# Layer 1's norms and features follow the gathering of expert results, its weights are prepared before the experts, and one edge input is read from PSUM

## The chip, the core and the metric

The kernel runs on one core of a Trainium2 chip. The core has five engines that each take their own instructions in order: TensorE (PE in the profile, with PEld for its weight loads), VectorE (DVE), ScalarE (ACT), GpSimd (POOL) and SyncE (SP), and 16 DMA engines that move data between the chip's memory and the core's two on-chip memories, SBUF and PSUM. The metric is the device time of one execution in microseconds (us), lower is better. The time before the change is 2966.57 us, the median of 3 runs (2961.47 to 2970.36).

## What is computed

A graph network of two layers over 3125 nodes with 256 features and 53125 edges. Each layer is a graph step and a feed-forward step, and each step adds to x what it makes of the normalised x:

```python
x = x + _L0_gnn_ref(_layernorm(x, axis=-1), edge_index, edge_weight, ...)   # 4 attention heads
x = x + _L0_ffn_ref(_layernorm(x, axis=-1)[None], ...)[0]                   # 16 experts, best 2 per node
x = x + _L1_gnn_ref(_layernorm(x, axis=-1), ..., src, dst, edge_type_200)   # 200 relations
x = x + _L1_ffn_ref(_layernorm(x, axis=-1)[None], ...)[0]                   # half of the nodes
```

Layer 0's graph step weighs each edge, per head, and takes a weighted mean over the edges of a node:

```python
score = a_s[:, src] + a_d[:, dst] + aw_e[:, None] * elem[None, :] + ab[:, None]
w = jnp.exp(-jax.nn.relu(score / 20.0))
pooled = jax.vmap(lambda wi, fi: seg(wi[:, None] * fi))(w, dst_f)
row_sum = jax.vmap(lambda wi: seg(wi))(w)
out = pooled / row_sum[:, :, None]
```

Layer 1's graph step has one weight per edge, made from both nodes and the edge's relation. The score's vector is the product of a 768 x 768 matrix W3 and a vector a. Since each alpha is divided by a sum over its own single entry, an edge's message is its source's features plus its relation's, times alpha / alpha:

```python
W = (W3 @ a)[:, 0]
score = h[src] @ w_src + h[dst] @ w_dst + rel_e @ w_rel
alpha = jnp.exp(jax.nn.leaky_relu(score))[:, None]
alpha = alpha / jnp.sum(alpha, axis=1, keepdims=True)
msg = (h[src] + rel_e) @ weight_neighbor * alpha
agg = jax.ops.segment_sum(msg, dst, num_segments=n)
node_repr = jax.nn.relu(agg) + loop_message
```

## The kernel before

Nodes lie in 25 tiles of 128 partitions; x (25 x 256 f32 per partition) stays in SBUF. Edges are sorted on the chip by target node, so that tile b of nodes owns 18 tiles of 128 edges (the last owns 8): 440 edge tiles, taken in 74 groups of six (GRP, the last of two). The program goes through these stages in order of time: sorting for layer 0; node features and edges of layer 0; sorting for layer 1, prepared; the experts, into which the moves of layer 1's sorting are woven; features of layer 1; edges of layer 1; the last feed-forward step.

A scheduler in the compiler orders the instructions of each engine from the program's order and a model of their times, and adds the waits. On the chip each engine then keeps its order: an instruction that waits holds all behind it on its engine. Buffers of a pool come free when their last user is done. Pools that are opened after others were closed lie in the memory that these left.

**Edges of a layer** (`edge_stages`, run by `pipelined` as a three-step pipeline over the groups):

- `gather`: GpSimd issues six indirect DMAs, one per edge tile, that fetch the rows of 128 edges from a table in DRAM into `rows`, which has three buffers (L733). VectorE makes the one-hot of the target node, `oh`, by comparing `iota` with the edges' target in its tile (L741), both read from SBUF. It also makes `hot` in bf16 by comparing `wide`, the same targets laid along the free axis and broadcast to all partitions, with the partition's number (L750). Layer 0 has one `hot` per group, layer 1 three (one for the target, two for the relation). `wide` is loaded once per node tile by SyncE, as one run of 18 x 128 values per partition (L722 to L725); layer 1 loads two.
- `message`: TensorE picks each edge's target score with `hot` (L759), VectorE sums the parts (L765), and then `messages` of the layer follows. Layer 0 (`heads_edges`): the score (L891 to L893), Exp on ScalarE into `msg` (L895), and the product of the row's 4 x 64 values with the four weights (L896), both inputs in SBUF. Layer 1 (`relations_edges`): the score (L1242), the weight, ScalarE's scaling of `oh` by it into `ohw` (L1251), and the one-hot of the relation, from `iota` and the edge's relation, both in SBUF, written beside the row (L1245).
- `add`: TensorE sums the group's messages into the tile's accumulator in PSUM, `ps_sum`, one of two buffers (L776). After a tile's last group VectorE takes it out (L784) and `finish` adds to x: L907 to L910 in layer 0; in layer 1 a chain over TensorE, ScalarE and VectorE (L1262 to L1287).

**Experts** (`experts`): norms of x, gate logits (L945), gating, 50 scatters of the nodes' places (L1014), then 65 tiles of work, each with its expert's weights loaded by SyncE. At the end GpSimd gathers for each node tile its two expert results, `yg` (L1102, six buffers), and VectorE adds them to x (L1106).

**Features of layer 1** (`relations_features`, called after the experts): W3 and a are loaded (L1130) and multiplied by rows, which gives W3 a (L1135); then the relation weights through TensorE (L1154 to L1185); then `layer_norm` of all 25 tiles (L149 to L156), whose Sqrt and reciprocal are one instruction each for all tiles and so need the last tile; then per tile two transposes, a copy, four matmuls and a copy into `f` (L167, L169, L1196, L1200), and one write to the table per five tiles (L1202).

## Time and profile before

| what | value |
|---|---|
| median of 3 runs | 2966.57 us |
| the profiled execution's own time | 2936.63 us |
| its span in the trace | 2934.5 us |
| TensorE, VectorE, GpSimd busy | 1868.3 us (64%), 1397.0 us (48%), 1416.7 us (48%) |
| gathers of rows (L733) | 880, mean 1118 ns |
| edges of layer 0, first to last gather's end | 397.1 to 1040.7 us |
| first expert's tokens gathered, last expert's result | 1335.8 to 1841.7 us |
| gathering of expert results | 1844.6 to 1906.9 us |
| edges of layer 1, first gather's start to last one's start | 1991.2 to 2636.9 us |

A line of the timeline gives the start in us from the span's start, the duration, the engine, the line of the program, the operation, its output and inputs, their shapes, how many were merged, and in brackets how long the engine sat idle before it and what ended that. A line of the chain of waits gives start, duration and what the program's end was waiting for then. In the table of stretches each engine has its busy time with the number of instructions in brackets, then the granted TensorE clock (1 is full), the share of the DMA engines that is busy, and GB/s. "issue" as the reason for a gap means that the engine waited for nothing that the profile shows.

### The profile page before, as it was taken

What the parts mean: (1) busy time and instruction counts of PE and PEld (TensorE: products, weight loads), DVE (VectorE), ACT (ScalarE), POOL (GpSimd) and SP (SyncE); (2) the same over time, 40 slices, a digit from 0 to 9 for tenths busy, and PEclk for the clock granted to TensorE, in tenths of its full rate; (3) what the DMA queues carried; (4) which work ended last, traced back from release to release, by engine and by line L of the source; (5) the groups of instructions that cost most, each with busy time, mean ns of one, the idle gap of its engine ahead of it and who ended that gap; (6) DMA issues with size and microseconds to landing.
All of it is one profiled execution on the core that took longest, in us unless ns stands there. A gap on an engine that the chain in (4) does not pass through costs nothing.

```text
span 2934.5 us, 24129 instructions
## 1 busy us (share of the span) xinstructions
PE 1868.3 (64%) x7420; PEld 1114.8 (38%) x7420; DVE 1397.0 (48%) x3320; ACT 368.6 (13%) x1008; POOL 1416.7 (48%) x1291
## 2 busy tenths in 40 slices
PE   3079644545455442406999999055877887786298
PEld 0024333333343310304666666042444444343166
DVE  4976344444444448423442222444555555548811
ACT  0000100000000000100002222011222222222012
POOL 4435247877777743154441111606777777760000
PEclk9999967766777755556779999587889888998599
DMA  2040144443444320004449998325555545530000
GB/s 80 0 128 5 35 130 119 117 120 111 122 117 117 100 74 0 1 0 152 127 128 314 314 317 280 93 88 165 147 148 146 149 137 148 148 101 33 7 20 17
DMA packets 185930, 334.13 MB, mean 114 GB/s; under 512 B 32733, under 2 KB 109799, under 8 KB 185799
## 3 DMA queue, kind: packets, MB, share of 16 engines
q1 hardware_dynamic: 122919, 191.33, 19.9%
q0 software_dynamic: 53520, 132.71, 17.0%
q10 hardware_dynamic: 9360, 8.52, 0.8%
q8 instruction: 60, 0.98, 0.1%
q14 instruction: 71, 0.58, 0.1%
HBM read 298.41 MB, written 34.04 MB: 113 GB/s over the span
## 4 chain that ended last, share of the span: by engine, by line
PE 29%; DVE 8%; POOL 7%; DMA 5%; issue 4%; ACT 1%; SPq 0%; DVEq 0%; ACTq 0%; POOLq 0%
PE ps_h L1062 8%; POOL rows L733 7%; PE ps_y L1079 4%; PE ps_sum L776 3%; DMA rows<-table,s_idx 3%; PE s_mv L550 3%; DVE cmp L1358 3%; PE ps_hid L1385 3%; PE ps_out L1396 2%; DMA yg<-ytab,moe_pi 1%; PE ps_h_t L167 1%; PE ps_loop L1275 1%; PE ps_f L1196 1%; DVE hot L750 1%; PE ps_x_t L167 1%
## 5 line engine op out<-in xcount | busy, mean ns | idle before, releaser
L733 POOL DMA_INDIRECT rows<-table,s_idx x880 | 983.5, 1118 | 462.5 <-issue 246.5
L776 PE MATMUL ps_sum<-rows,ohw 128*128 128x457 f32 x880 | 416.8, 618 | 117.1 <-ACT ohw L1251 116.8
L776 PE MATMUL ps_sum<-msg,oh 128*128 128x260 f32 x880 | 303.0, 519 | 135.0 <-DVE msg L896 135.0
L550 PE MATMUL s_mv<-s_hv,s_hp 128*128 128x200 f16 (+1 forms) x832 | 246.6, 471 | 88.5 <-DVE s_hv L545 88.5
L776 PEld LDWEIGHTS ps_sum<-msg,oh 128*128 128x128 f32 x880 | 229.1, 267 | 192.1 <-DVE msg L896 141.4
L776 PEld LDWEIGHTS ps_sum<-rows,ohw 128*128 128x128 f32 x880 | 173.7, 210 | 275.6 <-ACT ohw L1251 169.8
L1062 PE MATMUL ps_h<-w,x_t 128*128 128x512 f32 x520 | 255.4, 637 | 0.0
L1051 POOL DMA_INDIRECT xg<-xtab,who x65 | 62.0, 954 | 310.7 <-PE ps_x_t L167 295.0
L550 PEld LDWEIGHTS <-s_hp 128*128 128x128 f16 x832 | 121.9, 147 | 207.5 <-issue 91.8
L559 POOL DMA_INDIRECT s_tab<-s_rec,s_to x130 | 147.2, 1132 | 102.3 <-ACT s_rec L556 67.0
L891 DVE TENSOR_TENSOR s<-near,rows 128x24 f32<-128x24 f32 x74 | 13.5, 183 | 362.5 <-DMA rows<-table,s_idx 344.9
L741 DVE TENSOR_TENSOR oh<-iota,s_row 128x768 f32<-128x768 f32 (+1 forms) x148 | 138.6, 937 | 45.4 <-ACT ohw L1251 45.4
L759 PEld LDWEIGHTS <-hot 128*128 128x128 bf16 x1760 | 57.9, 98 | 269.3 <-DVE near L765 179.7
L1251 ACT ACTIVATE ohw<-oh,s 128x128 f32<-128x128 f32 x440 | 136.5, 389 | 105.3 <-DVE ln_mv L150 53.8
L759 PE MATMUL ps_near<-near0p,hot 128*128 128x12 bf16 x440 | 22.8, 174 | 198.7 <-DVE near L765 162.9
L1068 DVE TENSOR_TENSOR hid<-hid,ps_h 128x512 f32<-128x512 f32 x65 | 44.7, 687 | 210.6 <-ACT hid L1067 210.6
L1062 PEld LDWEIGHTS ps_h<-w,x_t 128*128 128x128 f32 x520 | 102.7, 209 | 104.7 <-issue 104.5
L437 POOL TENSOR_TENSOR s_pos<-s_pos,s_own 128x416 f32<-128x416 f32 x50 | 72.0, 1439 | 143.9 <-DVE s_own L434 124.5
L896 DVE TENSOR_TENSOR msg<-rows,msg 128x1536 f32<-128x1536 f32 x74 | 128.2, 1734 | 1.3 <-ACT msg L895 0.4
L1079 PE MATMUL ps_y<-w,h_t 128*128 128x256 f32 x520 | 122.9, 379 | 0.7 <-ACT h_t L169 0.7
L750 DVE TENSOR_SCALAR hot<-wide,pcols 128x768 bf16<-128x768 bf16 (+1 forms) x296 | 120.4, 423 | 3.3 <-DMA wide<-s_w 3.3
L1079 PEld LDWEIGHTS ps_y<-w,h_t 128*128 128x128 f32 x520 | 98.7, 190 | 41.7 <-issue 30.6
(293 smaller groups left out, 2495.7 us busy)
## 6 DMA issues: line engine op xcount, KB each, us to landing
w<-in_L_ffn_w_dram SPq DMA_DIRECT2D x195, 512.0 KB
wide<-s_w SPq DMA_DIRECT2D x72, 576.0 KB
rows<-table,s_idx POOLq DMA_INDIRECT x880
ytab<-y ACTq DMA_DIRECT2D x65, 128.0 KB
sums<-sums_z SPq DMA_DIRECT2D x5, 1142.5 KB
more<-sums SPq DMA_DIRECT2D x25, 228.5 KB
sums<-sums_z SPq DMA_DIRECT2D x5, 650.0 KB
table<-f SPq DMA_DIRECT2D x5, 650.0 KB
```

What stands on the lines that cost most here:

```text
L550: nc.tensor.matmul(ps[:, : NK * V], hp[:, :, j], rec[:, :, :, j].rearrange("p k v -> p (k v)"), start=(j0 + j == 0), stop=(j0 + j == C - 1),)
L559: d = nc.gpsimd.indirect_dma_start(out=tab, out_offset=bass.IndirectOffsetOnAxis(ap=to[:, i : i + 1], axis=0), in_=out[:, k * CH * V : (k ...
L733: nc.gpsimd.indirect_dma_start(out=rows[:, j, :width], out_offset=None, in_=table, in_offset=bass.IndirectOffsetOnAxis(ap=st["idx"][:, k + ...
L741: nc.vector.tensor_tensor(oh[:, :n, :], self.iota[:, None, :P].to_broadcast(sh), st["row"][:, k : k + n, None].to_broadcast(sh), op=OP.is_ ...
L750: nc.vector.tensor_scalar(t[:, : n * P], w, at, None, op0=OP.is_equal)
L776: nc.tensor.matmul(ps[:, :W], oh[:, j, :], msg[:, j, :], start=(head and j == 0), stop=(last and j == n - 1),)
L896: nc.vector.tensor_tensor(msg[:, :n, :HO].rearrange("p j (h o) -> p j h o", o=O), rows[:, :n, :HO].rearrange("p j (h o) -> p j h o", o=O), ...
L1062: nc.tensor.matmul(ph[:, i * HID : (i + 1) * HID], xt[:, c, :], w12[:, i, c, :], start=(c == 0), stop=(c == C - 1),)
L1079: nc.tensor.matmul(py[:, :D], ht[:, c, :], w3[:, c, :], start=(c == 0), stop=(c == HC - 1))
L1251: nc.scalar.activation(ow[:, j, :], oh[:, j, :], AF.Copy, scale=s[:, 1, j : j + 1])
L1358: nc.vector.tensor_scalar(cmp[:, s:e], wrow[:, s:e], w, None, op0=op, op1=OP.add, accum_out=rank[:, t, i : i + 1],)
L1385: nc.tensor.matmul(ph[:, : nt * P], w1[:, c, f * P : (f + 1) * P], zt[:, c, : nt * P], start=(c == 0), stop=(c == C - 1),)
```

## The change

Three edits go together.

**One edge input from PSUM.** `edge_stages` takes the two big PSUM buffers for the whole stage. `hold` gets a copy of the first 256 values of `iota` in its first bank (`numbers`) and in its second the edge weights of layer 0 (`weights_ps`); `sums2` holds the two accumulators, one bank each, by the tile's parity. `oh` and the one-hot of the relation compare `numbers`. In layer 0 ScalarE makes Exp twice, once into PSUM for the product and once into `msg`.

```diff
+        hold, sums2 = self.ps_a("ps_hold"), self.ps_a("ps_sums")
+        numbers = hold[:, :256]
+        nc.vector.tensor_copy(numbers, self.iota[:, :256])
+        self.numbers, self.weights_ps = numbers, hold[:, 512:]
...
-                oh[:, :n, :], self.iota[:, None, :P].to_broadcast(sh),
+                oh[:, :n, :], numbers[:, None, :P].to_broadcast(sh),
...
-                now["sum"] = self.ps_a("ps_sum")
+                now["sum"] = sums2[:, b % 2 * 512 : (b % 2 + 1) * 512]
...
+                w = self.weights_ps[:, : n * H].rearrange("p (j h) -> p j h", h=H)
+                nc.scalar.activation(w, s, AF.Exp)
                 nc.scalar.activation(msg[:, :n, HO:], s, AF.Exp)
...
-                    msg[:, :n, HO:, None].to_broadcast([P, n, H, O]), op=OP.mult,
+                    w[:, :, :, None].to_broadcast([P, n, H, O]), op=OP.mult,
...
-                    rows[:, :n, R0:], self.iota[:, None, :R].to_broadcast(sh),
+                    rows[:, :n, R0:], self.numbers[:, None, :R].to_broadcast(sh),
```

With it `wide` is laid in pieces of two edge tiles (256 values) with 8 values of room behind each, and `hot` is made from it in that form:

```diff
-            t = pool.tile([P, self.tiles[0] * P], BF16, name=f"wide{i}")
+            t = pool.tile([P, self.tiles[0] // 2, 2 * P + 8], BF16, name=f"wide{i}")
...
-                w = now[b][min(i, 1)][:, lo : lo + n * P]
-                t = pool.tile([P, G * P], BF16, name=f"hot{i}", bufs=3)
-                nc.vector.tensor_scalar(t[:, : n * P], w, at, None, op0=OP.is_equal)
+                w = now[b][min(i, 1)][:, lo : lo + n // 2, : 2 * P]
+                t = pool.tile([P, G // 2, 2 * P], BF16, name=f"hot{i}", bufs=3)
+                nc.vector.tensor_scalar(t[:, : n // 2, :], w, at, None, op0=OP.is_equal)
```

**Weights ahead of the experts.** `relations_features` becomes a generator. Its first part, up to the relation weights, is called after layer 1's sorting is prepared and before `experts`. W3 and a lie in a pool of their own that is closed at once; the pool of the features stays open through the experts.

```diff
-                self.experts(steps)
-        self.relations_features()
+                features = self.relations_features()
+                self.experts(steps, next(features))
+                next(features, None)
```

**Norms and features tile by tile.** `layer_norm` is split, so that `norm_tiles` makes the statistics, Sqrt, reciprocal and the normalised values of some tiles. `experts` calls `done(t)` after a tile's two additions, and at the ends of groups (4, 4, 4, 4, 4, 2 and 3 tiles) `done` makes norms, features and the table's write for the group.

```diff
+                done(t)
...
+            ends = list(range(4, NT - 4, 4)) + [NT - 3, NT]
+
+            def done(b):
+                if b + 1 not in ends:
+                    return
+                i = ends.index(b + 1)
+                t0, t1 = ends[i - 1] if i else 0, b + 1
+                self.norm_tiles(self.h1, t0, t1)
                 f = pool.tile([P, 5, D + 2], F32, name="f1")
-                n = min(5, NT - t0)
-                for t in range(t0, t0 + n):
+                for t in range(t0, t1):
...
+            yield done
```

## The prediction

> **What bounds the kernel now.** I read the table of stretches (busy time by engine) first: the two edge stages, 397 to 1041 us and 1991 to 2637 us, hold 44% of the span. Then GpSimd's own records there, one `rows` gather per 128 edges:
>
> ```profile
> core 0: us, POOL busy (x), PEclk, DMA share, GB/s
> 330.00:1050.00 720.00, 509.80 (x440) 0.71 0.39 112
> 1985.00:2640.00 655.00, 473.75 (x440) 0.87 0.51 144
> ```
>
> Both stages issue 440 gathers. The median gather takes 0.949 us, so 440 need 417.6 us. Layer 0 spends 92.2 us above that, layer 1 56.2 us. The timeline shows from whom:
>
> ```profile
> 2223.34 0.96 DVE L741 TENSOR_TENSOR oh<-iota,s_row 128x768 f32<-128x768 f32 x1 [1.90 <-ACT ohw L1251]
> 2224.22 0.63 DVE L784 TENSOR_TENSOR acc<-ps_sum,more 128x457 f32<-128x457 f32 x1
> 2224.76 1.40 DVE L1245 TENSOR_TENSOR rows<-iota,s_val 128x1200 f32<-128x1200 f32 x1
> ...
> 2223.98 1.14 POOL L733 DMA_INDIRECT rows<-table,s_idx  x1 [0.30 <-issue]
> 2225.42 1.56 POOL L733 DMA_INDIRECT rows<-table,s_idx  x1 [0.30 <-issue]
> ```
>
> See the ends. The gather begun at 2223.98 ends at 2225.12, 0.82 us after `oh` ended (2224.30). The next ends at 2226.98, 0.82 us after the compare of L1245 (2226.16). A gather that begins inside a VectorE operation with two SBUF inputs starts its work when that ends. L784 has one PSUM and one SBUF input. It ran 2224.22 to 2224.85, across the first gather's start of work, and did not hold it: held, the gather would have ended at 2225.67. That is the row for this change.
>
> In layer 0 GpSimd alone sets the pace: from 400 to 1000 us, 124.3 of the 124.6 us of gaps before gathers are "issue", 0.30 us each. In layer 1 it is not alone: about 55 us of gaps wait for VectorE or TensorE.
>
> Between the stages the chain of waits gives a serial stretch:
>
> ```profile
> 1898.39 2.79 DMA yg<-ytab,moe_pi
> 1902.14 2.79 DMA yg<-ytab,moe_pi
> 1905.90 2.67 DMA yg<-ytab,moe_pi
> 1911.04 7.78 DVE xn L156 x24
> 1918.87 5.37 DVE w3a L1135 x12
> 1925.22 1.80 PE ps_rw L1162 x4
> 1927.67 1.82 PE ps_rw L1162 x4
> 1978.76 3.93 DMA table<-f
> ```
>
> Gathering of expert results, all norms, W3 times a, relation weights, then 25 feature tiles: the last addition to x ends at 1909.15, the last table write issues at 1978.76. That is 69.6 us with GpSimd idle.
>
> **1. One input from PSUM, layer 0.** `oh` (74 times, 0.94 us) and `msg` (74, 1.73 us) get one PSUM input, so by L784 they hold no gather. Still with two SBUF inputs: L909 and L910 (0.41 us per tile each), L891 and L892 (0.18 and 0.16 per group). A gather starting at random inside one of length d waits d/2, with chance d/1.25: 0.067 us per 0.41 us operation, 3.3 us for 49 of them, and 1.7 us for the small ones. Saved: 92.2 - 5 = **87 us** (74 if I am wrong about a fifth, 92 at most). What is late next: a group's gathers then take 7.5 us, VectorE's work 4.0 us (44% of 8.95), TensorE's 4.6; rows has three buffers, so neither is near.
>
> [...] L784 at 260 wide takes 413 ns, L910 at 256 wide, all SBUF, 412. I take 0[...]. ScalarE's second Exp (74 at 0.22 us) finds an engine 2% busy; VectorE waits for the first of the pair, as now.
>
> **2. The same in layer 1.** Here a latency loop decides. A tile's first group takes TensorE from 2195.25 to 2206.65, 11.4 us without a gap, because the finish of the tile before is interleaved. Its rows buffer goes to the next tile's first group: gathers 2206.93 to 2214.7 (7.8 us), landed 2217.99, weights to 2221.35 and TensorE at 2221.90, 26.6 us on. GpSimd waits 1.6 to 2.6 us per tile for that buffer. Freed gathers shorten the loop only by this group's contention, 7.9 to 7.5 us in the tiles I read; the rest becomes a longer wait for the buffer. Against it stands one slower `hot` in the loop (part 3), 0.2 us. Net -0.3 us for 24 tiles: **-7 us**. If the loop did not bind, all 56 us would go; I take the loop.
>
> **3. `hot` and its padded input.** No row shows the new pattern. [...] The source is now 3 x 256 with gaps. [...] Kept: 409 ns as now. Refused: the rows 128x768 (409) and 128x256 (278) give 0.256 ns per element, and half the rate adds 197 ns. On 222 operations in layer 1 that is 44 us of VectorE, in layer 0 (74) 15 us, beside gathers except the one in the loop. I take refused. [...]
>
> Each `wide` copy now lands in 512 B runs. Queue rows: q10 moves 910 B packets in 0.8% of 16 engines (40 ns each), q1 1557 B packets in 76 ns. Two copies per tile are 2304 runs, 144 per engine: 3.2 us at q10's time per byte, 5.8 us at 40 ns per run, against 3.5 now. Per layer-1 tile that is -0.3 to +2.3 us, in a burst (2211 to 2217) under the loop's last gather. q10 is no dearer per byte, so 0; end +55 us.
>
> **4. Weights ahead of the experts.** W3 now loads into the buffers of the finished sorting, and the experts' own tiles lie where W3 was. Before:
>
> ```profile
> 1199.96 0.38 SPq L508 DMA_DIRECT2D s_buckets<-s_bki  x1
> 1208.97 0.37 SPq L928 DMA_DIRECT2D gw<-in_L_ffn_gate_w_dram  x1
> ```
>
> SyncE's gate-weight load waits 9 us for that memory; TensorE, idle 94 us behind it, starts the logits at 1213.07. Logits (27 us), gating, and 50 scatters of 1.26 us follow in series to the first expert, with nothing to hide a shift. In the new order: W3's load (1909.35 to at most 1918.87, 9.5 us), six multiplies to 1924.2, then gw: +14.8 us. SyncE's queue holds W3, a, wx and two `re` loads ahead of gw. The relation matmuls ended 22.0 us after W3's issue; if TensorE keeps them in front, the logits start 17.9 us later. I take **+16 us** (0 if the experts' tiles lie clear of W3, 18).
>
> **5. Norms and features follow the gathering.** GpSimd's 50 gathers (947 ns + 0.30) are 62.6 us, 2.50 us per tile. VectorE per tile by start-to-start times: two additions 0.82, stats 0.49, normalise 0.33, feature copy 0.43, shares of reciprocal and near 0.12, together 2.19 us. It fits, with 0.3 us to spare. Contention: 0.38 x 0.24 us per gather, 4.6 us, and normalising 1; I take 6 us. TensorE: 1.87 us per tile at granted clock 0.99, but the clock in this stretch was 0.51, where transposes took 0.60 instead of 0.38 us and the 256-wide relation matmuls 2.0; so up to 3 us for each of the last three tiles. After the last addition: stats 0.6, Sqrt and reciprocal 1.0, first normalise 0.4, three tiles 9, copies and issue 0.7, together 12 us. 69.6 - 12 - 6 = **-52 us** (-36 to -60). The table's own landing and the record load behind it stay.
>
> **Sum.** -87 - 7 + 16 - 52 = -130 us. The profiled execution took 2936.63 us (span 2934.5 and 2 around it): 2807. The median shown is 2966.57, 1.0% above it, so -131 there: **2835 us**.
>
> **Rivals.**
> A. VectorE becomes the bound while gathering: its queue is in order, and each feature copy waits out a 1.87 us tile. For: 0.3 us slack, six yg buffers. Against: in the trace stats are already woven between additions. 25 x 3.6 = 90 us + 12 saves 30 instead of 52: **2857**.
> B. Layer 1 lengthens: 512 B runs at the dear end plus `hot` in the loop, +62 us instead of the -7. For: the loop. Against: q10. **2900**.
> C. Layer 1's loop does not bind, its 56 us go: **2785**.
> D. Slower. [...] all nine per tile sit on layer 1's loop, 5.3 us, with 2.3 us for the runs: 7.6 x 24.4 = 185 us. It decides from 5.6 us per tile; **about 3026**. Against: runs of 256 adjacent elements, and only one `hot` seen in the loop.
> That the change doesn't do what it says: PSUM next to a broadcast SBUF input might hold gathers still. L784 and L1281 argue against; it falls within D's share.
>
> **Chances.** Forecast 0.50, A 0.17, B 0.15, C 0.06, D 0.12 (a quarter of it within 0.3%, what a measurement here can tell from no change). Faster 0.88, same 0.03, slower 0.09. Range: C and the cheap ends below (2790), B above: 2910. D is left out.
>
> **What would show it.** Right: layer 0's gathers nearly all 0.95 us, its stage near 555 us long; `hot` near 606 ns; GpSimd waiting longer for `rows` in layer 1; gate weights loaded 15 us after the memory is free; the last table write 12 to 20 us after the last addition. Wrong: gathers still ending 0.82 us after `msg`, layer-1 tiles leaving 26 us either way, or additions waiting for feature copies.

## The result and the profile after

The changed kernel takes 2983.76 us (median of 6 runs, 2976.39 to 2995.04). The kernel before, run beside it, takes 2967.39 us (6 runs). The ratio is 1.0062 with a 95% interval of 1.0038 to 1.0087: **slower by 0.6%**. The profiled execution took 2982.18 us, its span 2978.5. The forecast was 2835.

Here are the stages of the two profiled executions, in us. A stage of edges runs from its first `rows` gather to the end of its last. `xg` is the first tile that the experts load, `yg` the first gathering of expert results. The 397 us ahead of layer 0's edges are the same in both.

| stage | before | after | difference |
|---|---|---|---|
| edges, layer 0 | 643.6 | 683.2 | +39.6 |
| to the first `xg` (weights moved here) | 295.1 | 305.3 | +10.2 |
| experts, to the first `yg` | 508.8 | 506.6 | -2.2 |
| `yg` to layer 1's first `rows` gather | 146.6 | 111.3 | -35.3 |
| edges, layer 1 | 647.0 | 678.2 | +31.2 |
| after layer 1's last gather | 296.4 | 296.9 | +0.5 |

The stage that should have lost most of the time gained some. Yet GpSimd's own records in it are as forecast. This is the view of stretches for GpSimd in the changed kernel, over the two edge stages; the columns are the stretch, its length, GpSimd's busy time with the number of instructions, the granted clock, the share of the DMA engines and the rate.

```profile
core 0: us, POOL busy (x), PEclk, DMA share, GB/s
330.00:1090.00 760.00, 419.92 (x440) 0.70 0.38 106
1995.00:2690.00 695.00, 416.05 (x440) 0.86 0.52 135
```

Against 509.80 and 473.75 before, the contention is gone: 440 gathers take 420 and 416 us, 0.95 us each. But the stages contain 263 and 262 us in which GpSimd does nothing. In layer 0 the view of waits says for whom (columns: the waiting instruction, its releaser; total us, number, longest):

```profile
POOL rows L747 <- DVE msg L913: 132.7, 16, 8.6
POOL rows L747 <- issue: 127.9, 417, 1.1
```

"issue" is the 0.30 us per gather that was there before. New are 16 waits of about 8.3 us for `msg`, the last reader of a `rows` buffer. So VectorE was late with `msg`. What VectorE waits for is the next view:

```profile
DVE oh L755 <- remote: 244.7, 22, 17.4
DVE s L906 <- DMA rows<-table,s_idx: 80.4, 23, 5.4
DVE acc L799 <- remote: 24.8, 4, 7.5
DVE oh L755 <- PE ps_sums L791: 18.1, 8, 6.3
```

`oh` of a group has three buffers. It can start when TensorE's sums (L791) three groups earlier have read that buffer. "remote" means that the trace has a semaphore event for the release but no engine's work that ended close to it. The timeline shows what that is (columns: start, duration, engine, line, operation; in brackets the idle time before it and the releaser):

```profile
675.39 1.75 DVE L913 TENSOR_TENSOR msg<-rows,ps_hold 128x1536 f32<-128x1536 f32 x1
677.29 4.39 PE L791 MATMUL ps_sums<-msg,oh 128*128 128x260 f32 x12 [2.47 <-DVE msg L913]
...
686.10 0.95 POOL L747 DMA_INDIRECT rows<-table,s_idx  x1 [0.30 <-issue]
691.66 0.96 DVE L755 TENSOR_TENSOR oh<-ps_hold,s_row 128x768 f32<-128x768 f32 x1 [14.52 <-remote]
```

VectorE ended `msg` at 677.14. TensorE heard of it at once: it started the sums at 677.29, 0.15 us later. The sums that this `oh` waits for are those of an earlier group and had ended at 674.82, before `msg` even began. **VectorE went on at 691.66, 16.84 us after that end**, and 4.6 us after GpSimd had run out of buffers and stopped (its last gather ended at 687.05). Behind `oh` in VectorE's order stood the work that would have given GpSimd its buffer.

By this view it is no wait for an engine's work: TensorE's message that it is done arrives late. (Starts of matmuls are recorded, their ends are modelled, so the trace can't tell a late message from a last matmul that finished late.) In layer 0 of this execution `oh` and `near` wait 32 times for TensorE. Counted from the moment when both the matmul and VectorE's own previous work had ended, these waits make 246 us, 24 of them over 1 us and up to 15.0. The 23 of `oh` among these start 6.6 to 22.0 us after the sums' end. In layer 1 it is `near`:

```profile
DVE near L780 <- remote: 107.4, 24, 9.9
```

In the profile that the prediction was read from there is none of this: in its layer 1 the 22 waits of `near` start at most 0.08 us after the matmul's end, and in its layer 0 neither `oh` nor `near` waits for TensorE.

A second thing is new, and nothing in the forecast allowed for it. The two accumulators in PSUM were two buffers and are now two halves of one, `sums2`. Before, TensorE ran from one tile's sums into the next tile's while VectorE had yet to take out the finished one (`acc`; its buffer is then free). Here are such a change of tile before (24 matmuls are two groups, of two tiles, without a break) and one in the changed kernel (run e12, below):

```profile
594.61 8.39 PE L776 MATMUL ps_sum<-msg,oh 128*128 128x260 f32 x24 [1.66 <-DVE msg L896]
603.02 0.41 DVE L784 TENSOR_TENSOR acc<-ps_sum,more 128x260 f32<-128x260 f32 x1
```

```profile
596.45 0.42 DVE L799 TENSOR_TENSOR acc<-ps_sums,more 128x260 f32<-128x260 f32 x1
597.02 4.75 PE L791 MATMUL ps_sums<-msg,oh 128*128 128x260 f32 x12 [1.76 <-DVE acc L799]
```

In all 24 changes of tile of layer 0 the changed kernel's next sums start 0.14 to 0.15 us after `acc` ends, in the recorded run as in e12. Before, they started 0.3 to 5.8 us ahead of that end, all 24 times. So a TensorE that waits for VectorE's `acc` now stands in a ring with a VectorE that waits for TensorE's sums, once per tile. Every kernel below with the PSUM inputs has this ring.

### The profile page after: what moved, and what is told of

Its sections match the earlier page's. It is cut to its first block, busy times and chain, and to the rows that moved or that the text cites. A ratio compares the mean times of both kernels' runs of the same rounds, so it can differ in the third digit from the quotient of the medians.

```text
span 2978.5 us, 24253 instructions
## 1 busy us (share of the span) xinstructions
PE 1884.8 (63%) x7420; PEld 1116.8 (37%) x7420; DVE 1438.6 (48%) x3330; ACT 377.1 (13%) x1088; POOL 1268.6 (43%) x1291
## 5 line engine op out<-in xcount | busy, mean ns | idle before, releaser
L747 POOL DMA_INDIRECT rows<-table,s_idx x880 | 836.0, 950 | 626.6 <-issue 234.6
L791 PE MATMUL ps_sums<-rows,ohw 128*128 128x457 f32 x880 | 417.9, 622 | 61.9 <-ACT ohw L1280 51.1
L791 PE MATMUL ps_sums<-msg,oh 128*128 128x260 f32 x880 | 299.2, 509 | 166.8 <-issue 87.2
L791 PEld LDWEIGHTS ps_sums<-msg,oh 128*128 128x128 f32 x880 | 222.7, 260 | 219.1 <-issue 154.2
L755 DVE TENSOR_TENSOR oh<-ps_hold,s_row 128x768 f32<-128x768 f32 (+1 forms) x148 | 140.0, 946 | 291.4 <-remote 244.7
L791 PEld LDWEIGHTS ps_sums<-rows,ohw 128*128 128x128 f32 x880 | 180.5, 217 | 219.2 <-issue 158.0
L764 DVE TENSOR_SCALAR hot<-wide,pcols 128x768 bf16<-128x768 bf16 (+1 forms) x296 | 173.7, 592 | 69.6 <-PE ps_near L773 51.4
L773 PEld LDWEIGHTS <-hot 128*128 128x128 bf16 x1760 | 67.5, 98 | 359.8 <-DVE hot L764 214.5
L913 DVE TENSOR_TENSOR msg<-rows,ps_hold 128x1536 f32<-128x1536 f32 x74 | 128.3, 1733 | 0.4
L541 DVE TENSOR_TENSOR s_hp<-num_p,s_pp 128x1024 f16<-128x1024 f16 x104 | 71.8, 690 | 82.7 <-PE s_mv L556 81.2
```

Of the source, the lines that this page charges most:

```text
L747: nc.gpsimd.indirect_dma_start(out=rows[:, j, :width], out_offset=None, in_=table, in_offset=bass.IndirectOffsetOnAxis(ap=st["idx"][:, k + ...
L755: nc.vector.tensor_tensor(oh[:, :n, :], numbers[:, None, :P].to_broadcast(sh), st["row"][:, k : k + n, None].to_broadcast(sh), op=OP.is_equal,
L764: nc.vector.tensor_scalar(t[:, : n // 2, :], w, at, None, op0=OP.is_equal)
L773: nc.tensor.matmul(pe[:, j * 3 * nv : (j + 1) * 3 * nv], t[:, j // 2, j % 2 * P : (j % 2 + 1) * P], v.rearrange("p q v -> p (q v)"), start ...
L791: nc.tensor.matmul(ps[:, :W], oh[:, j, :], msg[:, j, :], start=(head and j == 0), stop=(last and j == n - 1),)
L913: nc.vector.tensor_tensor(msg[:, :n, :HO].rearrange("p j (h o) -> p j h o", o=O), rows[:, :n, :HO].rearrange("p j (h o) -> p j h o", o=O), ...
```

## The experiments

The letters in the expectations below name the theories of the time at which each was written; every set of kernels that was run together has its own runs of the kernel before beside it. For each run the median, that of the kernel before, and the ratio with its 95% interval are given.

**First set: the parts alone.** e1 has only the weights ahead of the experts and the norms and features tile by tile; e2 only the PSUM inputs with the padded `wide`; e3 is the changed kernel with the old form of `wide` and `hot`; e4 lets GpSimd write a scratch tile after the six gathers of each group, so that the row of gathers has a gap.

```diff
# e1_moves: of the change, only
+                features = self.relations_features()
+                self.experts(steps, next(features))
...
+                done(t)
```

> The kernel before with the moved parts alone (norms and features follow the gathering, weights ahead of the experts); edge stages untouched. My theory (the loss sits in the edge stages): layer 0's gathers take 644 us and layer 1's 647 as before, expert results' first gather to layer 1's first gather 111 us instead of 147, weights +5 to +8; together -28 us, ratio 0.990. Rival (the moved work disturbs the edge stages, through memory or order): layer 1's gathers take over 665 us here too, ratio 1.00 or more.

```diff
# e2_edges: of the change, only
+                oh[:, :n, :], numbers[:, None, :P].to_broadcast(sh),
...
+                    w[:, :, :, None].to_broadcast([P, n, H, O]), op=OP.mult,
```

> The kernel before with the edge part alone (inputs from PSUM and the padded wide copies). My theory: both edge stages as in the changed kernel, 683 and 678 us, VectorE waiting for TensorE's results up to 17 us after these end; +70 us, ratio 1.024. Rival (the moved work disturbs the edge stages): they take under 650 us each here, ratio under 1.00.

```diff
# e3_oldwide: against the changed kernel
-            t = pool.tile([P, self.tiles[0] // 2, 2 * P + 8], BF16, name=f"wide{i}")
+            t = pool.tile([P, self.tiles[0] * P], BF16, name=f"wide{i}")
...
-                t = pool.tile([P, G // 2, 2 * P], BF16, name=f"hot{i}", bufs=3)
+                t = pool.tile([P, G * P], BF16, name=f"hot{i}", bufs=3)
```

> The changed kernel with the wide copies and hot in their old, unpadded layout; PSUM inputs and moves stay. Theory W (TensorE's completions are held up when gathers follow each other without a break): hot (0.41 us, one per group in layer 0, three in layer 1) breaks the row of gathers only a little; late waits of VectorE for TensorE remain, at least half of layer 0's 246 us; layer 0 650 to 690 us. Rival R (the 512-byte runs of the padded copies hold them up): the late waits are gone, layer 0's gathers take 560 to 590 us, the whole under 2900 us, ratio 0.97.

```diff
# e4_pause: against the changed kernel, after a group's gathers
+            rest = pool.tile([P, 512], F32, name="rest", bufs=1)
+            nc.gpsimd.memset(rest, 0.0)
```

> The changed kernel with a GpSimd memset of 128x512 (about 0.5 us, with its gap 0.8) after the gathers of each group; nothing else changes. Theory W: the break lets TensorE's completions through, late waits shrink to under a third, layer 0's gathers take 610 to 630 us in place of 683, layer 1 under 660, so adding work makes the kernel faster: ratio 0.96 to 0.98. Rival R or any cause that has nothing to do with the row of gathers: layer 0 683 or more, the whole 0 to 60 us longer than the changed kernel, ratio 1.006 to 1.03.

| kernel | us / before | ratio | edges 0 | `yg` to edges 1 | edges 1 |
|---|---|---|---|---|---|
| e1_moves | 2936.35 / 2966.48 | 0.9888 [0.9853, 0.9924] | 644.8 | 110.8 | 676.5 |
| e2_edges | 3011.49 / 2966.48 | 1.0134 [1.0109, 1.016] | 681.0 | 153.2 | 676.4 |
| e3_oldwide | 2971.34 / 2966.48 | 1.0017 [0.9999, 1.0036] | 665.9 | 111.1 | 686.1 |
| e4_pause | 2977.53 / 2966.48 | 1.0041 [1.0024, 1.0058] | 658.0 | 111.0 | 695.6 |

What follows: the moves gain 1.1% and the edge part loses 1.3%. The 512 B runs of the padded `wide` are not the cause, since without them layer 0 still takes 665.9 us with some 220 us of late signals. A gap of 0.53 us in each group makes the lateness less (some 160 us instead of 246) and layer 0 25 us shorter, but layer 1 is 17 us longer, and no saving in time can be told where 2 to 4% were expected. And e1 holds a surprise: its layer 1 is that of the kernel before, instruction for instruction, and takes 676.5 us, not 647. Something lengthened that stage which is not in the change.

**Second set: the kernel before, looked at again, and more buffers.** e5 is the kernel before, unchanged. e6 gives `oh`, `hot` and `msg` six buffers in layer 0, so that VectorE waits for sums of six groups ago. e7 is e1 with four `rows` buffers. e8 is the changed kernel with layer 0 fetching 64 of each row's 260 values and with the messages' contents left out (they are zeros).

> The kernel before, unchanged, profiled beside the other runs. Its profile shown so far took 2936.6 us where its timed runs take 2966. My theory: in the timed runs TensorE's completions are late in layer 1 here too (as in the run of the moves alone), so this profile shows 2960 to 2970 us, layer 0's gathers 644, layer 1's about 676 in place of 647, and over 100 us of late waits of VectorE for TensorE in layer 1. Rival (the moves lengthened layer 1 in their run): layer 1 takes 647 here, and the 30 us lie elsewhere.

```diff
# e6_deep: against the changed kernel, in layer 0 only
-            oh = pool.tile([P, G, P], F32, name="oh", bufs=3)
+            oh = pool.tile([P, G, P], F32, name="oh", bufs=self.deep)
# the same for hot and msg0; self.deep is 6 in layer 0 and 3 in layer 1
```

> The changed kernel with six buffers in place of three for oh, hot and msg in layer 0; nothing else. If late completions cost only because VectorE needs an oh buffer back from TensorE (theory W1): VectorE no longer waits at oh, layer 0's gathers take 560 to 610 us, ratio 0.97 to 0.98. If completions are let through at a limited pace per gather (theory W2), the wait only moves to the next thing that needs TensorE (near, acc): layer 0 stays at 640 to 690 us, ratio 1.00 to 1.006.

```diff
# e7_rows4: against e1_moves, the tile of the gathered rows
-bufs=3
+bufs=4
```

> The moved parts alone (edge stages as before) with a fourth rows buffer in both layers. If layer 1 is bound by the loop through the rows buffer, as the prediction took it: layer 1's gathers fall from 676 to 610-640 us, ratio about 0.97. If the late completions themselves set layer 1's pace, whatever the buffers: layer 1 stays within 10 us of 676, ratio 0.989.

```diff
# e8_narrow: against the changed kernel, in layer 0; rows are tiles of zeros made beforehand
+            rows = kept[g % 3]
...
+                    out=rows[:, j, :64], in_=view
```

> The changed kernel, but layer 0's gathers fetch 64 columns in place of 260 (the other columns of rows stay zero, so layer 0's messages are left out); same number of gathers, same instructions otherwise. If the late completions come with the bytes the gathers move: late waits of VectorE for TensorE in layer 0 fall under 30 us (246 in the changed kernel), gathers take 555 to 590 us. If they come with the number of gathers, or with GpSimd's issue alone: late waits stay over 150 us, gathers 640 us or more.

| kernel | us / before | ratio | edges 0 | edges 1 |
|---|---|---|---|---|
| e5_before | 2981.95 (one run) / 2972.12 | | 649.0 | 680.9 |
| e6_deep | 3070.01 / 2972.12 | 1.0294 [1.0237, 1.035] | 669.4 | 773.4 |
| e7_rows4 | 2979.7 / 2972.12 | 1.0016 [0.9997, 1.0034] | 645.0 | 702.5 |
| e8_narrow | 3034.89 (one run) / 2972.12 | | 687.5 | 704.6 |

e5 matters most. It is the kernel before, and its profile is not the one that the prediction was read from. GpSimd's stretch and VectorE's waits in layer 1:

```profile
core 0: us, POOL busy (x), PEclk, DMA share, GB/s
1995.00:2690.00 695.00, 475.26 (x440) 0.89 0.47 136
```

```profile
DVE near L765 <- PE ps_sum L776: 76.7, 31, 5.0
...
DVE near L765 <- remote: 22.4, 5, 10.5
```

The gathers are as busy as in the first profile (508.78 against 509.80, 475.26 against 473.75), but layer 1 takes 680.9 us instead of 647.0. In the first profile `near` waited 6.6 us there in 22 waits, the longest 0.3. Late signals cost this kernel 104 us of waits of `near` in layer 1 and 8.7 us of waits of `oh` in layer 0, where it hardly ever waits for TensorE. So the lateness is older than the change. The timings of before (2961 to 2972 us) fit a kernel that has it, and the one profile read for the prediction (2936.63) had not.

e6 moves the wait instead of removing it. In layer 0 of e6:

```profile
DVE near L780 <- remote: 90.3, 11, 15.0
DVE acc L799 <- remote: 69.6, 5, 21.0
```

`oh` is gone from the list, and the next instructions that need TensorE in the same group stand in its place. Six buffers only shift which signal is waited for. Why layer 1, with the same instructions in the same order as in the changed kernel, grew to 773.4 us (182.5 us of waits of `hot` for "remote" from 2050 to 2650 us) stays open, and with it the ratio of 1.0294 where at most 1.006 was expected. The recorded run shows how held signals come free: its layer 1 has 23 bursts of five updates by TensorE, 0.042 us apart, each in a pause of the gathers and 2.3 to 3.3 us after the last one's end. That fits signals held up by the row of gathers, but doesn't prove it, since GpSimd itself waits for TensorE there.

The amount of data is not the cause: with a quarter of the bytes (e8, one run) layer 0 takes 687.5 us and has some 220 us of late signals. A fourth `rows` buffer makes the moves alone slower where a gain or no change was expected: layer 1 takes 702.5 us in e7 and 676.5 in e1.

**Third set: break the row of gathers.** If the gain of the PSUM inputs is what leaves no gap for the signals, some contention should be given back on purpose: `oh` from SBUF again, or `msg`'s weights from SBUF again, or a longer pause.

```diff
# e9_oh_sbuf: against the changed kernel
-                oh[:, :n, :], numbers[:, None, :P].to_broadcast(sh),
+                oh[:, :n, :], self.iota[:, None, :P].to_broadcast(sh),
```

> The changed kernel with oh reading its numbers from SBUF again (two SBUF inputs, 0.95 us, once per group); msg and the relation compare keep PSUM. Theory W2 (the more the row of gathers is broken, the sooner TensorE's completions get through; pace settles between them): the mean gather in layer 0 rises from 0.954 to about 1.02 us, late waits fall from 246 to 150-200, layer 0's gathers take 655 to 675 us in place of 683; ratio 1.000 to 1.004. Rival (the PSUM reads themselves hold TensorE up): each input taken out of PSUM takes its share of the late waits away, layer 0 under 620.

```diff
# e10_msg_sbuf: against the changed kernel
-                nc.scalar.activation(w, s, AF.Exp)
...
-                    w[:, :, :, None].to_broadcast([P, n, H, O]), op=OP.mult,
+                    msg[:, :n, HO:, None].to_broadcast([P, n, H, O]), op=OP.mult,
```

> The changed kernel with msg reading its weights from SBUF again (two SBUF inputs, 1.73 us, once per group, and no second Exp); oh and the relation compare keep PSUM. W2: msg breaks the row of gathers for longer than oh does (mean gather 1.06 us), late waits fall under 120 us, layer 0's gathers take 645 to 660 us; ratio 0.996 to 1.001. Rival (PSUM reads hold TensorE up): as for oh, layer 0 under 620.

```diff
# e11_pause_long: against e4_pause
-            rest = pool.tile([P, 512], F32, name="rest", bufs=1)
+            rest = pool.tile([P, 1300], F32, name="rest", bufs=1)
```

> The changed kernel with a longer GpSimd pause after each group's gathers (memset of 128x1300, 1.19 us, with its gap 1.5; the shorter one was 0.53, with its gap 0.83). W2: late waits in layer 0 fall again (246 without, 162 with the short pause, under 110 with this), but gathers and pauses alone already take 550 + 74 x 1.5 = 661 us, so layer 0 takes 665 to 680 us: no length of pause brings it under the 644 to 649 us of the kernel before. Ratio 1.004 to 1.012. Rival (a fixed hold-up that a long enough pause clears): 661 to 663 us and no late waits over 1 us left.

| kernel | us / before | ratio | edges 0 | edges 1 |
|---|---|---|---|---|
| e9_oh_sbuf | 2811.26 / 2936.02 | 0.9566 [0.9533, 0.9598] | 570.4 | 625.1 |
| e10_msg_sbuf | 2855.75 / 2936.02 | 0.9737 [0.9698, 0.9776] | 619.7 | 616.7 |
| e11_pause_long | 2923.21 / 2936.02 | 0.9945 [0.9923, 0.9967] | 630.7 | 678.0 |

All three are faster than before, and none of the three has a late signal. That looks like a cure, but the time of the kernel before warns: beside them it is itself at 2936.02 and not at 2966 to 2972, and nothing was done to it. So this set says nothing yet about the edits, and it doesn't test their expectations, which were made for late signals. The changed kernel itself has to be run in the same set.

**Fourth set: the changed kernel again, unedited, beside two that were measured before.** e13 is e9 and e14 is e1.

> The changed kernel itself, unchanged. The kernel before took 2966 to 2972 us beside the first eight runs, whose traces show TensorE's completions late, and 2936 us beside the last three, whose traces show none late. Theory C (late completions are a property of the chip that the run falls on; where they are absent the prediction's sum holds): beside a before of about 2936 us this takes 2790 to 2830 us, ratio 0.950 to 0.965, layer 0's gathers 555 to 570, layer 1's 610 to 630; beside a before of about 2968 it repeats 1.006 with 683 and 678. Rival (oh's read of PSUM holds TensorE up on any chip; the last three runs were fast because of their edits): ratio 1.00 or more whatever the kernel before takes, with late waits of VectorE for TensorE over 150 us in layer 0.

> The kernel of e9_oh_sbuf again (oh's numbers from SBUF). Theory C: beside a before of about 2936 us 0.957 again; beside a before of about 2968 us late waits of 120 to 220 us in layer 0, its gathers 650 to 680 us, ratio 0.99 to 1.004. Rival (oh's read of PSUM holds TensorE up): 0.955 to 0.965 whatever the kernel before takes.

> The kernel of e1_moves again (moved parts alone). Theory C: the edge stages lose what late completions cost there; beside a before of about 2936 us layer 0 644, layer 1 640 to 650, the moved stretch -40, ratio 0.985 to 0.989; beside a before of about 2968 us 0.989 again with layer 1 at 676.

| kernel | us / before | ratio | edges 0 | `yg` to edges 1 | edges 1 |
|---|---|---|---|---|---|
| e12_after | 2777.26 / 2931.08 | **0.9485 [0.9464, 0.9507]** | 552.0 | 98.9 | 613.3 |
| e13_oh_sbuf | 2804.09 / 2931.08 | 0.9558 [0.9527, 0.959] | 567.4 | 99.2 | 618.0 |
| e14_moves | 2888.46 / 2931.08 | 0.9871 [0.984, 0.9903] | 643.4 | 98.7 | 643.7 |

The same program that took 2983.76 us takes 2777.26 here, and the kernel before takes 2931.08. The stretches of e12:

```profile
core 0: us, POOL busy (x), PEclk, DMA share, GB/s
330.00:955.00 625.00, 418.31 (x440) 0.74 0.45 129
1855.00:2480.00 625.00, 416.65 (x440) 0.88 0.55 151
```

The gathers' own busy time is that of the recorded run to 0.4% (418.31 against 419.92, 416.65 against 416.05). Only what lies between them differs. The waits of VectorE in layer 0, and one release on the timeline:

```profile
DVE s L906 <- DMA rows<-table,s_idx: 204.3, 53, 7.6
DVE oh L755 <- PE ps_sums L791: 36.8, 21, 2.5
```

```profile
604.74 4.31 PE L791 MATMUL ps_sums<-msg,oh 128*128 128x260 f32 x12 [2.97 <-DVE msg L913]
...
609.09 0.96 DVE L755 TENSOR_TENSOR oh<-ps_hold,s_row 128x768 f32<-128x768 f32 x1 [1.23 <-PE ps_sums L791]
```

Here VectorE waits for the gathered rows, as it should behind GpSimd, and `oh` starts 0.04 us after the sums end (604.74 + 4.31 = 609.05), not 17 us after. Of GpSimd's 131.9 us of waits in layer 0, 130.1 are "issue". The 21 waits of `oh` fit the ring of the accumulators: all fall on the second group of a tile, and the kernel before had none. While signals are prompt they cost GpSimd nothing that shows.

**Fifth set: do four `rows` buffers or an `oh` from SBUF help where the signals are late?** e15 is the changed kernel with `rows` at `bufs=4` as in e7, e16 is e9, e17 is the changed kernel.

> The changed kernel with a fourth rows buffer. Where completions are not late (a before of about 2931 to 2936 us beside it): if the loop through the rows buffer still bounds layer 1 (GpSimd waited 63 us for TensorE to give rows back), layer 1's gathers fall from 613 to 555-580 us, layer 0 stays at 552, ratio 0.930 to 0.940; if TensorE itself is the bound by now (497 us busy in 614), layer 1 stays over 595, ratio 0.943 to 0.949. Where they are late (a before of about 2968): layer 1 at 680 or more, since a longer row of gathers holds completions up for longer; ratio 1.00 or more.

> The kernel of e9_oh_sbuf again, for its time where completions are late: beside a before of about 2968 us late waits of 120 to 220 us in layer 0, its gathers 650 to 680 us, ratio 0.99 to 1.004; beside a before of about 2931 to 2936 us 0.956 once more.

> The changed kernel again, in the same surroundings as the two above: 0.9485 where the kernel before takes 2931 to 2936 us, 1.006 where it takes about 2968.

| kernel | us / before | ratio | edges 0 | edges 1 |
|---|---|---|---|---|
| e15_after_rows4 | 2997.5 / 2966.59 | 1.0097 [1.0059, 1.0135] | 679.4 | 672.8 |
| e16_oh_sbuf | 3001.24 / 2966.59 | 1.01 [1.0022, 1.0178] | 674.7 | 698.7 |
| e17_after | 2986.58 / 2966.59 | 1.0067 [1.0047, 1.0087] | 684.3 | 678.4 |

This set has late signals again: before is back at 2966.59 and the changed kernel gives 1.0067, the recorded 1.0062. The `oh` edit that stood at 0.9566 is at 1.01. Its layer 0, in the view of VectorE's waits of e16:

```profile
DVE oh L755 <- remote: 158.0, 15, 17.6
```

So e9's gain was the gain of the PSUM inputs on `msg` in surroundings where signals are prompt; `oh`'s contention given back neither cures the lateness nor is it free (e13 is 27 us slower than e12). e10 and e11 were not run where signals are late. In the recorded run's layer 0, 16 of the 23 late `oh` start in a pause of GpSimd, 3.2 to 4.9 us after its last gather, and the pauses tried are shorter than that (0.53 us in e4; 1.19 in e11, by a memset of the same shape in the kernel before, its L309), so whether a longer pause helps is open. The fourth `rows` buffer changes nothing that can be told from e17.

**What all sets say together.** The sets fall into two kinds by the kernel before alone: 2966 to 2972 us (the recorded comparison, sets one, two and five) and 2931 to 2936 us (sets three and four, and the profile that the prediction was read from). In the first kind signals from TensorE come late in layer 1 of every profile taken, and in layer 0 of every kernel with the PSUM inputs; in the second kind they are late nowhere. The changed kernel is 0.6 to 0.7% slower in the first kind and 5.15% faster in the second; the moves alone are 0.9888 in the first kind and 0.9871 in the second. What makes a set one or the other lies outside the kernel and is **open**. One and the same chip ran sets one and four, and another sets three and five, each falling once on either side, so the lateness doesn't belong to a chip.

One mark goes with it. In the profiles of the second kind the trace holds about 16 updates of the gathers' own semaphores per gather, in those of the first kind 2 to 10; it is 15.8 and 15.6 in the two edge stages of the profile that the prediction was read from, 3.2 and 4.5 in those of the recorded run. Updates by VectorE and ScalarE are missing too: the recorded run holds 2356 of 2921 and 665 of 969, the first profile 2953 of 2963 and 935 of 937. Whether the missing records are a trace of the same disturbance or the recording has a part in it can't be told from these runs, since the timed executions are recorded too, each with its span and clock.

## Why the prediction was wrong

Each step is set against both kinds: against the profile it was read from, e12 (signals prompt) is the like-for-like measurement; against e5, the recorded run (signals late). The late column adds up to -2 us and the medians to +16, since e5 is a single execution, 15 us above the median of before in the recorded comparison.

| step | forecast | prompt: e12 - first profile | late: after - e5 |
|---|---|---|---|
| 1. layer 0 edges | -87 | -91.6 | +34.2 |
| 2. layer 1 edges | -7 | -33.7 | -2.7 |
| 4. weights ahead | +16 | +10.5 (to the first `yg`; +9.3 to the first `xg`) | +9 |
| 5. norms and features | -52 | -47.7 | -42.1 |

**Step 1 is the one that failed**, in one clause: "What is late next: ... rows has three buffers, so neither is near." It asked how long VectorE's and TensorE's work takes per group (4.0 and 4.6 us against 7.5) and found room. It put at nothing the time that the word from TensorE takes to reach VectorE, because the profile showed at most 0.08 us. In the recorded run it is up to 22 us from the end of the matmul. It also took the two accumulators for independent, which they no longer are; even with prompt signals `oh` waits for TensorE 21 times in layer 0 of e12. In the first profile neither happened, and even e5, with late signals, lost only 8.7 us of waits of `oh` there (and 13.0 of `hot` and `acc`): the contended gathers kept GpSimd the later one. The change takes this cover away and adds the ring. VectorE now reaches `oh` before the sums three groups back are reported, stands there, and holds `msg` behind it.

The 89 us by which the gathers got shorter and another 34 go into GpSimd's 132.7 us of waits. That late signals are needed for the loss is shown, since the same program gains where they are prompt. How much of it is the lost cover and how much the ring is not: no kernel with the PSUM inputs and two separate accumulators was run.

Where signals are prompt the step holds within 5 us, with its mechanism: gathers of 0.951 us, stage 552.0 against the forecast 555. The PSUM source costs next to nothing, as taken: at equal shapes `oh` takes 951 to 954 ns (944 from SBUF), `msg` 1746 to 1748 (1748), the relation compare 1398 (1397).

**The scaling to the median hid the sign of it.** The profiled execution was 30 us below the timings shown, and the prediction only multiplied the sum by 1.01. e5's execution, 45 us above the first profile, tells where such us sit: 34 in layer 1 (680.9 against 647.0), where the late signals are, 5 in layer 0 and 7 between `yg` and layer 1's edges. A profile faster than all timings was the visible hint that the time has a part which this profile doesn't show.

**Step 2** was right in the mechanism and too small. In the prompt case layer 1 lost 33.7 us, about midway between the 7 taken and rival C's 56: the loop through the `rows` buffer does bind. The view of GpSimd's waits in e12's layer 1 has

```profile
POOL rows L747 <- PE ps_sums L791: 62.9, 23, 9.3
```

that is 2.7 us on average in 23 waits, about one per change of tile. But the loop itself got shorter, by 33.7 / 24.4 = 1.4 us per tile instead of the 0.3 taken from the tiles read: the contention of the loop's own group was mis-sized. Over all tiles the six gathers of a tile's first group take 8.14 us before and 7.20 in e12, which is 0.94 of the 1.4; the rest was not traced. In the late case the 2.7 us that layer 1 gained over e5 can't be told from nothing.

**Step 3**, `hot` came out at the slower of the two times weighed (409 and 606 ns), as taken:

```profile
L764 DVE TENSOR_SCALAR hot<-wide,pcols 128x768 bf16<-128x768 bf16 x292 | 172.6, 596 | 69.6 <-PE ps_near L773 51.4 <-PE ps_sums L791 15.9 <-DMA wide<-s_w 2.3
```

596 ns was 606 in the forecast, by the slope of two rows. In layer 1 of the recorded run 768 values take 592 ns and 256 take 312, which is 0.55 ns per value where the rows of before, 409 and 278, gave 0.256. That the padded form would go at half the rate was the prediction's estimate; why it does was not shown. The 512 B runs cost nothing that shows: the mean gather is 0.946 us in layer 1, and e3 without them has no shorter layer 1 (686.1 against 678.2). Rivals B and D fall with that.

**Step 4** came out at +10 instead of +16, by another sum than the one made. The recorded run, SyncE's queue:

```profile
1242.12 0.38 SPq L514 DMA_DIRECT2D s_buckets<-s_bki  x1
...
1252.47 0.37 SPq L1152 DMA_DIRECT2D w3a<-in_L_gnn_W_dram  x1
...
1268.54 0.37 SPq L945 DMA_DIRECT2D gw<-in_L_ffn_gate_w_dram  x1
```

The gate weights are issued 26.4 us after `s_buckets` instead of 9.0: 17.4 us later, close to the 14.8 to 17.9 worked out; the stage up to `s_buckets` took 2.7 us more and the way from the load to the first logit 3.9 more. What gave 13.6 us back is the logits behind them. They ran from 1276.5 to 1292.5, 16 us, instead of 29.6 (1213.0 to 1242.6), a matmul taking 263 instead of 374 ns at a granted clock of 1.00 instead of 0.50. The relation matmuls now stand just ahead of them; that these are why the clock was up wasn't tried.

**Step 5** was right in kind, -42 and -48 for -52, and TensorE was the term that was mis-sized. In e12, TensorE in this stretch:

```profile
1801.40 2.09 PE L1223 MATMUL ps_f<-wx,x_t 128*128 128x258 f32 x4 [0.52 <-ACT x_t L175]
...
1804.44 2.09 PE L1223 MATMUL ps_f<-wx,x_t 128*128 128x258 f32 x4 [0.52 <-ACT x_t L175]
```

A tile takes 1804.44 - 1801.40 = 3.04 us, at a granted clock of 0.53 from 1797 to 1830 (0.50 in the recorded run), while a tile of expert results comes every 2.50. The forecast took 1.87 us, at a clock of 0.99, for all but the last three tiles. So TensorE bounds the stretch, together with the 0.52 us per tile that it waits for ScalarE's copy, and not VectorE as in rival A.

**The sum** for the prompt case is -154 (2777.26 - 2931.08) where -131 was forecast; the profiled executions differ by 162.5 (2774.08 and 2936.63), of which the four steps make 162.5. For the recorded comparison it is +16. No rival described that: D put the slower case at 3026 by an estimated 590 ns more for each `hot` (three times the 197 worked out from the two rows; 183 came in layer 1), and the 9 in 100 for slower stood for that mechanism, which did not come. A wait for a completion that comes later than the work ends was in none of them, nor was a TensorE that waits for `acc`.

**Which version to keep.** Where signals are prompt, the changed kernel is the fastest that was run (0.9485). Where they are late, it is slower than before, and the moves alone are the best (0.9888). The moves alone gain 1.1 to 1.3% in both kinds, so without knowing the surroundings they are the safe choice. No kernel here was better than both in both kinds, and neither four `rows` buffers where signals are prompt nor two separate accumulators were tried with the PSUM inputs.

## What to carry to other kernels

Compare the profiled execution's time with the timed runs before building a sum on it: a profile that is faster than all of them (here 2936.63 against 2961.47 at the least) may have left something out, and a second profile is cheap beside a wrong sum. When a change frees the engine that sets the pace, list the waits of each in-order engine that its slowness covered, with the number of buffers between them; the price of such a wait is that of the signal's arrival (up to 22.0 us in the recorded run) as well as of the work. When two buffers become halves of one, look in the trace for a wait between them. And before an edit is credited with a gain, run the unedited kernel in the same set.

## What the runs showed of the hardware

- In the sets of the first kind TensorE's completions reach VectorE late: 23 of the 74 `oh` in layer 0 of the recorded run start 6.6 to 22.0 us after the (modelled) end of the matmul, where the same program's 22 waits in e12 start 0.04 us after it. Of these 23, 16 come while GpSimd's gathers pause and 7 while they go on. In layer 1, bursts of five arrive 0.042 us apart, 23 times, each in a pause of the gathers. VectorE's signal to TensorE took 0.15 us in the same stretch.
- This depends on something outside the program: the kernel before takes 2931 or 2967 us by it, the changed one 2777 or 2984. With a quarter of the bytes per gather it is there all the same (e8).
- With the row of gathers broken by 0.53 us in a group the lateness was less (some 160 against 246 us), but no time was saved that can be told; deeper buffers moved the wait to another instruction (e6), cost time (e7) or did nothing that can be told (e15).
- With one input of `oh` and `msg` read from PSUM in place of SBUF, the mean gather of layer 0 went from 1.159 us to 0.954 in the recorded run and 0.951 in e12, and the two operations took 10 ns more at most.
